# Layer 2's listed tiles in groups with one common range of nodes, added in PSUM by TensorE

## The chip, the cores and the metric

The kernel runs on one core of a Trainium2 chip. The metric is the time of one launch in device microseconds (us), the median of several runs. The profile is of one further execution, which has a time of its own.

## The reference

A two-layer relational graph convolution with 10 relations, a residual and a layer norm, in float32. There are N = 12,500 nodes with C = 128 features and E = 200,000 edges, sorted by their target `dst`. An edge's relation is the argmax of 10 of its 42 attributes. The weight of an edge's message is one over the number of edges with its target and relation.

```python
def _rgcn_layer(x, src, dst, edge_type, w_rel, root, bias):
    N = x.shape[0]
    seg = dst * NUM_REL + edge_type
    xs = x[src]
    sums = jax.ops.segment_sum(xs, seg, num_segments=N * NUM_REL)
    cnt = jax.ops.segment_sum(jnp.ones(seg.shape, x.dtype), seg, num_segments=N * NUM_REL)
    mean = (sums / jnp.maximum(cnt, 1.0)[:, None]).reshape(N, NUM_REL, -1)
    return jnp.einsum('nrd,rdo->no', mean, w_rel) + x @ root + bias

edge_type = jnp.argmax(msg[:, NODE_EMB_DIM:-NODE_EMB_DIM], axis=1)
h = jax.nn.relu(_rgcn_layer(x, src, dst, edge_type, w_rel1, root1, b1))
out = _layernorm(x + _rgcn_layer(h, src, dst, edge_type, w_rel2, root2, b2))
```

## The kernel before

Edges are cut into 1563 tiles of 128. **Layer 1** gathers each tile's source rows with an indirect DMA from GpSimd (L814), builds a one-hot tile on VectorE (`hots`, L821), whose row is an edge, whose column is a pair of node and relation in a short window of nodes, and whose entry is the edge's weight. TensorE multiplies the two (L1058) and VectorE adds the window into an accumulator of sums (`sum_into`, L847) at an offset that it loads into a register (`offsets`, L832). A finished block of 256 nodes is projected. Layer 1 also gathers the new features of source nodes that are already finished and sums them for layer 2 in the same way; these sums wait in DRAM (`SD`).

**Layer 2** (`layer_2`) does what is left. For each finished node and relation a projected row lies in `YD`. First come 177 plain tiles, whose edges are used as they stand. Behind them come the *listed* tiles: of each of 127 rows of 11 tiles, only the edges whose source was not finished in time in layer 1 are left, and `brought_together` packs them on the chip, while the plain tiles run, into 678 tiles of 128 edges (`NT2`). `listed(c)` makes, for each chunk of 128 such tiles, the gather's indices `idxB`, the keys `keyB` (an edge's node minus its tile's first node), the weights `wB` and the tiles' first nodes `rowB`. A tile's edges span a number of nodes that the planner bounds by `width2(u)`, from the share of edges left (`dense`, 0.92 down to 0.08); a tile that spans more raises a flag, and a general path at the end computes everything anew. The list has two runs, tiles 0 to 488 and 489 to 677; `taken_in_turns` merges them by a debt (`owed`).

The work runs in *bunches* of up to four tiles, in an order fixed when the program is built (`bunches`). For bunch `p` the code issues:

- the one-hot tiles of bunch `p + AH` (three ahead) on VectorE, in one of seven buffers;
- a gather for each tile of bunch `p` on GpSimd, into six buffers `g` of eight tiles each (`gathers`); the order in a buffer turns round on each use, so the first gather into it waits for the last product of its former use;
- the products of bunch `p` on TensorE (L1570), each tile into columns of its own of one of five PSUM banks (`zy0` to `zy2`, `zq0`, `zq1`);
- the adds of bunch `p - BE` (two behind) into `acc2` on VectorE (L1599), one per tile, each at its own register offset, which is loaded for eight tiles at a time and set by a register step ("ISA", FUSED_REGOPS).

Between them lie: the saved sums of 46 blocks, loaded by SyncE (1280 KB each, two buffers) and projected by ten products into the bank `alone` (`seen`, L807), then added by VectorE (L1494); `begun` (L1470), which starts a block of `acc2`; and `finish`, which transposes a finished block on TensorE (L1504), adds `x` (L754), normalizes and stores. A block is finished as soon as the adds of the last bunch that can touch it are issued. All engines take their instructions in the written order.

Of the kernel before, what the change touches and what calls it, by code (L numbers as in the profile page):

```python
# [9 lines left out]
F32 = mybir.dt.float32  # L10
BF16 = mybir.dt.bfloat16
I32 = mybir.dt.int32
# [8 lines left out]
P = 128  # L21
# [3 lines left out]
WN = 12  # L25
KW = NREL * WN
WMAX = 120
G = 16
QB = 4
GB = 6  # L30
# [10 lines left out]
YB = 512  # L41
# [26 lines left out]
def rgcn_resnorm_kernel(ctx: ExitStack, tc: tile.TileContext, x, src, dst, attr, w_rel1, root1, b1,  # L68
# [120 lines left out]
    def width2(u):  # L189

        a, b = rows_at(u, extent[u >= UX])
        w = max(row_width(r) for r in range(a, b + 1))
        assert w <= WMAX
        return w

    const = ctx.enter_context(tc.tile_pool(name="const", bufs=1))
    dram = ctx.enter_context(tc.tile_pool(name="dram", bufs=1, space=DRAM))
# [1115 lines left out]
    def listed(c):  # L1313
# [17 lines left out]
        nc.tensor.transpose(ps[:, :p], s_f[:p], ident[:p, :p])  # L1331
        nc.vector.tensor_scalar(si[:p], ki[:p], 4, None, op0=ALU.arith_shift_right)
        b = comp.tile([P, 4], F32, name="bB")
        bi = comp.tile([P, 1], I32, name="biB")

        def by_tile(to, vals):
            nc.vector.memset(to, float(vals[0]))
            for i in range(1, p):
                if vals[i] != vals[i - 1]:
# [3 lines left out]
        nc.vector.tensor_reduce(b[:p, 0:1], si[:p], axis=AX.X, op=ALU.max)  # L1343
        nc.vector.tensor_scalar(b[:p, 0:1], b[:p, 0:1], reach_of[1][:p, c:c + 1], reach_of[0][:p, c:c + 1],
                                op0=ALU.max, op1=ALU.min)
        nc.vector.tensor_scalar(bi[:p], b[:p, 0:1], -1.0, float(TOPN), op0=ALU.mult, op1=ALU.add)
        nc.scalar.dma_start(rowB[:, u0:u0 + p], bi[:p])
        key = comp.tile([P, P], F32, name="keyb")
        nc.vector.tensor_scalar(key[:p], si[:p], -1.0, b[:p, 0:1], op0=ALU.mult, op1=ALU.add)
        yield 1  # L1350
        nc.vector.tensor_copy(idxB[:, u0:u0 + p], ps[:, :p])
# [3 lines left out]
        nc.vector.tensor_scalar(v[:p], la[:p], 0.5, None, op0=ALU.is_gt)  # L1355
        nc.vector.tensor_tensor(dn[:p], key[:p], v[:p], op=ALU.mult)
        nc.vector.tensor_reduce(b[:p, 1:2], dn[:p], axis=AX.X, op=ALU.max)
        by_tile(b[:, 2:3], [width2(u) - 0.5 for u in range(u0, u0 + p)])
        nc.vector.tensor_tensor(b[:p, 1:2], b[:p, 1:2], b[:p, 2:3], op=ALU.is_gt)
        nc.vector.tensor_tensor(fl[:p], fl[:p], b[:p, 1:2], op=ALU.max)  # L1360
        nc.vector.tensor_scalar(li[:p], li[:p], P - 1, None, op0=ALU.bitwise_and)
# [20 lines left out]
    def layer_2():  # L1382

        def units(a, b):
            u, r = a, []
            while u < b:
                w = width2(u)
                n = 1
                while u + n < b and n < min(QB, YB // w) and width2(u + n) == w:
                    n += 1  # L1390
                r.append((True, u, n, w))
                u += n
            return r

        walks = [units(0, UX), units(UX, NT2)]

        def taken_in_turns(mean):
            rest = [list(walk) for walk in walks]
            order = []
            while sum(u[2] for u in order) < LEAD:  # L1400
                order.append(rest[0].pop(0))
            end = []
            while sum(u[2] for u in end) < LAST:
                end.insert(0, rest[0].pop())
            owed = 0.0
# [124 lines left out]
        for p in range(-AH, NB + BE):  # L1530
# [21 lines left out]
            if p < NB:  # L1552
                second, t0, n, w = bunches[p]
                oh = ohs.pop(p)
                zps[p] = zp = next_of("zp", banks)
                for j in range(n):
                    if made % GQ == 0:
                        g = next_of("g", gathers)
                        turn = used_[id(g)] = 1 - used_.get(id(g), 1)
                    at = GQ - 1 - made % GQ if turn else made % GQ  # L1560
                    made += 1
                    t = t0 + j
                    if second:
                        gathered(g, at, YD[:, :], idxB[:, t:t + 1], 1)
                    else:
                        gathered(g, at, YD[:NREL * (limit_of(t) + 1), :] if t >= T0 else YD[:, :], idxE[:, t:t + 1], 1)
                    gs[j] = g, at
                for j in range(n):
                    g, at = gs.pop(j)
                    nc.tensor.matmul(zp[:, j * w:(j + 1) * w], g[:, at * C:(at + 1) * C], oh[:, j * w:(j + 1) * w],  # L1570
                                     start=True, stop=True)
                i = issued[p + 1]
            if flag is None and i >= NG - 28 * QB:
                assert not jobs.due
# [8 lines left out]
                    seen_in(j)  # L1583
            for q in [q for q in sorted(zps) if q <= p - (1 if p >= NB - 4 else BE)]:
                second, t0, n, w = bunches[q]
                for j in range(n):
                    t = t0 + j
                    if (second, t) not in offs:
                        if second:
                            m = min(GB2, (UX if t < UX else NT2) - t)  # L1590
                            assert {t // P, (t + m - 1) // P} <= ready
                            vals = offsets(rowB[:, t:t + m], t, m, bounds2, False)
                        else:
                            m = min(GB2, (NX if t >= T0 else T0) - t)
# [4 lines left out]
                    nc.vector.tensor_tensor(s, s, zps[q][:, j * w:(j + 1) * w], op=ALU.add)  # L1599
# [177 lines left out]
```

## Time and profile before

| | |
|---|---|
| time, median of 3 runs | 3716.18 us (3711.78 to 3717.28) |
| time of the profiled execution | 3674.72 us |
| its span, first to last instruction | 3672.9 us |
| mean granted TensorE clock | 0.747 |
| busy: PE, DVE, ACT, POOL | 62%, 56%, 14%, 62% |
| listed tiles' gathers, first to last start | 2639.9 to 3629.3 us |
| gathers of listed tiles | 678, mean 947 ns |

PE is TensorE's matmul, PEld its weight load, DVE VectorE, ACT ScalarE, POOL GpSimd, SP SyncE; a name with a q is an engine's sequencer. A row of a group of instructions gives line, engine, operation, tiles (out<-in), shapes and count, then busy time and the mean of one in ns, then the engine's idle time just before them and what ended it. A row of the timeline gives start and duration, and in brackets the idle time before it. "issue" means that the engine waited for nothing that the profile shows, "remote" that the releaser is not in it. A row of the waits gives who waited for whom, the total in us, the times and the longest.

### The profile page before, as it was taken

To read this page: it belongs to the slowest core of one execution; us is meant where nothing else is said; L and a number is where in the kernel's file an instruction comes from. 1 tells how busy PE (TensorE), PEld (TensorE's weight loads), DVE (VectorE), ACT (ScalarE), POOL (GpSimd) and SP (SyncE) were. 2 spreads that over 40 slices of the span, in tenths; PEclk is the share of its full clock that TensorE was granted. 3 is DMA by queue.
4 is the path that set the end of the run, shared out by engine and by line. 5 is a ranking of instruction groups with operands and counts; after the bars stand their busy time and mean duration, and the time that the engine had idled before them with its cause. 6 is when DMAs were issued, how large, how long until landed. Compare 5 with 4: busy or idle time off the path is not lost.

```text
span 3672.9 us, 39395 instructions
## 1 busy us (share of the span) xinstructions
PE 2278.8 (62%) x11107; PEld 1884.6 (51%) x11107; DVE 2042.8 (56%) x6834; ACT 514.7 (14%) x799; POOL 2293.4 (62%) x2430
## 2 busy tenths in 40 slices
PE   1557676767676767666667677633556567666533
PEld 0445555555555655555555555523455456555533
DVE  4646576767565756575656565438653234333344
ACT  1111121212121212121212121100000000000000
POOL 5664666666666666666666666566566666666663
PEclk7677887888888888888888877855667666776655
DMA  4553655455555555555555555531234444444321
GB/s 121 156 166 100 191 158 189 151 190 160 187 165 176 171 171 174 170 173 174 178 174 174 161 162 160 149 82 52 70 103 138 134 132 145 141 145 133 86 61 43
DMA packets 377189, 529.35 MB, mean 144 GB/s; under 512 B 56664, under 2 KB 284467, under 8 KB 376964
## 3 DMA queue, kind: packets, MB, share of 16 engines
q0 software_dynamic: 99552, 249.45, 23.7%
q1 hardware_dynamic: 249209, 264.48, 22.2%
q10 hardware_dynamic: 28203, 12.82, 1.2%
q8 instruction: 92, 1.51, 0.2%
q14 instruction: 133, 1.09, 0.1%
HBM read 372.75 MB, written 160.19 MB: 145 GB/s over the span
## 4 chain that ended last, share of the span: by engine, by line
PE 18%; DVE 12%; issue 11%; another core or an unknown queue 9%; POOL 1%; DVEq 1%; ACT 1%; DMA 0%; SPq 0%; POOLq 0%; ACTq 0%
PE alone L807 5%; PE zp L1058 4%; DVE oh L821 3%; DVE cc L1599 3%; PE zy L1570 2%; PE pf L807 2%; PE yb L915 2%; POOL g L814 1%; PE zq L1570 1%; DVE cc L847 1%; DVEq L832 1%; DVE cc L1261 1%; PE pf L1296 1%; DVE go L1249 0%
## 5 line engine op out<-in xcount | busy, mean ns | idle before, releaser
L814 POOL DMA_INDIRECT g<-XH,idxE x1386 | 1313.9, 948 | 737.8 <-issue 364.9
L1058 PEld LDWEIGHTS zp<-oh,g 128*128 128x128 f32 x5898 | 901.9, 230 | 399.0 <-DVE cc L847 177.1
L1058 PE MATMUL zp<-oh,g 128*128 128x120 f32 x5898 | 943.4, 317 | 238.5 <-DVE cc L847 135.2
L847 DVE TENSOR_TENSOR cc<-cc,zp 128x240 f32 (+1 forms) x1563 | 606.5, 388 | 791.3 <-remote 317.6
L814 POOL DMA_INDIRECT g<-YD,idxB x678 | 641.9, 947 | 348.8 <-issue 193.2
L915 PE MATMUL yb<-w,a 128*128 128x512 f32 (+1 forms) x576 | 347.9, 694 | 343.4 <-ACT ys L921 176.7
L821 DVE TENSOR_SCALAR oh<-bank,keyE,wE 128x120 f32<-128x120 f32 x1563 | 517.5, 393 | 0.0
L807 PE MATMUL alone<-cc,w 128*128 128x256 f32 (+2 forms) x920 | 302.9, 498 | 93.9 <-issue 64.1
L1570 PE MATMUL zy<-oh,g 128*128 128x12 f32 (+20 forms) x1158 | 217.6, 324 | 198.7 <-DVE cc L1599 124.2
L921 ACT ACTIVATE ys<-yb 128x512 f32<-128x512 f32 (+2 forms) x291 | 153.0, 526 | 1325.4 <-remote 534.1
L1570 PEld LDWEIGHTS zy<-oh,g 128*128 128x128 f32 x1158 | 222.4, 278 | 210.7 <-DVE cc L1599 128.4
L807 PEld LDWEIGHTS alone<-cc,w 128*128 128x128 f32 x920 | 233.7, 270 | 147.3 <-issue 75.5
L915 PEld LDWEIGHTS yb<-w,a 128*128 128x128 f32 x576 | 110.6, 239 | 377.6 <-ACT ys L921 198.3
L807 PE MATMUL pf<-cc,w 128*128 128x256 f32 (+2 forms) x1040 | 247.1, 395 | 17.1 <-issue 8.3
L814 POOL DMA_INDIRECT g<-in_x_dram,idxE x177 | 167.6, 947 | 134.9 <-PE zp L1058 62.6
L814 POOL DMA_INDIRECT g<-YD,idxE x177 | 168.4, 951 | 114.7 <-issue 59.7
L807 PEld LDWEIGHTS pf<-cc,w 128*128 128x128 f32 x1040 | 205.3, 211 | 50.8 <-issue 15.7
L776 ACT ACTIVATE cc<-zero 128x1280 f32<-128x1280 f32 x170 | 214.5, 1262 | 0.0
L1599 DVE TENSOR_TENSOR cc<-cc,zy 128x12 f32 (+22 forms) x579 | 102.5, 177 | 181.1 <-remote 87.9
L821 DVE TENSOR_SCALAR oh<-columns,keyB,wB 128x15 f32<-128x15 f32 (+26 forms) x678 | 159.6, 319 | 0.0
L754 DVE TENSOR_TENSOR cc<-pf,x 128x256 f32<-128x256 f32 (+2 forms) x52 | 21.2, 408 | 227.2 <-remote 94.2
L1570 PE MATMUL zq<-oh,g 128*128 128x15 f32 (+26 forms) x552 | 98.6, 319 | 63.6 <-issue 28.4
(257 smaller groups left out, 1567.8 us busy)
## 6 DMA issues: line engine op xcount, KB each, us to landing
SD<-cc SPq DMA_DIRECT2D x41, 1280.0 KB
cc<-SD SPq DMA_DIRECT2D x41, 1280.0 KB
YD<-ys SPq DMA_DIRECT2D x194, 256.0 KB
m<-in_edge_attr_dram SPq DMA_DIRECT2D x48, 672.0 KB
g<-XH,idxE POOLq DMA_INDIRECT x1386
YD<-ys SPq DMA_DIRECT2D x97, 128.0 KB
XH<-hb SPq DMA_DIRECT2D x44, 256.0 KB
g<-YD,idxB POOLq DMA_INDIRECT x678
```

Of the source, the lines that this page charges most:

```text
L776: nc.scalar.activation(cc[:, l, h * H:(h + 1) * H, o:o + n], zero[:, None, :n].to_broadcast([P, H, n]), AF.Copy)
L807: nc.tensor.matmul(po[:, :n], wsb[l][:, r, :], sums[:, r], start=(r == 0), stop=(w is None and r == NREL - 1))
L814: nc.gpsimd.indirect_dma_start(out=g[:, j * C:(j + n) * C], out_offset=None, in_=table, in_offset=bass.IndirectOffsetOnAxis(ap=idx, axis=0))
L821: nc.vector.tensor_scalar(oh[:, j * m:(j + 1) * m], cols[:, :m], keys[:, j:j + 1], weights[:, j:j + 1], op0=ALU.is_equal, op1=ALU.mult)
L832: vals = nc.values_load_multi_w_load_instructions(row, engines=[DVE], min_val=min(a for a, _ in lims), max_val=max(b for _, b in lims), sk ...
L847: nc.vector.tensor_tensor(s, s, z, op=ALU.add)
L915: nc.tensor.matmul(yb[:h, :m], fin_a[k][:, b * P:b * P + h], wsb[1][:, r:r + m // C, :], start=True, stop=True)
L921: nc.scalar.activation(ys[:h, :m], yb[:h, :m], AF.Copy)
L1058: nc.tensor.matmul(zp[:, o + l * KW:o + (l + 1) * KW], g[:, (slot[j] + l) * C:(slot[j] + l + 1) * C], oh[:, j * KW:(j + 1) * KW], start=Tr ...
L1261: nc.vector.copy_predicated(to[:, c - m:EW - m], go[:, c - KW:], a[:, c:])
L1570: nc.tensor.matmul(zp[:, j * w:(j + 1) * w], g[:, at * C:(at + 1) * C], oh[:, j * w:(j + 1) * w], start=True, stop=True)
L1599: nc.vector.tensor_tensor(s, s, zps[q][:, j * w:(j + 1) * w], op=ALU.add)
```

## The change

`group_at` joins listed tiles that follow each other into groups of four, else of two, else one, where the group's common range of nodes fits 120 columns: 38.6 over the smallest `dense` plus 2.99 for four, 20.8 for two, the old width for one. A group is a bunch. All its tiles have one first node, the group's, and one width; TensorE adds the group's products in the same columns of PSUM, and VectorE adds the columns once. `listed` therefore finds the group's first node across tiles, which lie in partitions: a transpose to one partition, a maximum over each group, a copy back over the group, and a small matmul back to partitions. `rowB` is now written by VectorE, where a DMA of ScalarE's queue did it. Two more steps of `QB` tiles lie in `listed`. The debt of the merge counts the add once per bunch.

```diff
+GROUPS = ((4, 38.6), (2, 20.8))
...
+    def group_at(u, end):
+
+        for n, m in GROUPS:
+            if u % P + n <= P and u + n <= end:
+                a, b = rows_at(u, extent[u >= UX])[0], rows_at(u + n - 1, extent[u >= UX])[1]
+                if a:
+                    w = int(m / min(dense[a * RT:(b + 1) * RT]) + 2.99)
+                    if w <= WMAX:
+                        return n, w
+        return 1, width2(u)
+
+    groups2, u = [], 0
+    while u < NT2:
+        n, w = group_at(u, UX if u < UX else NT2)
+        groups2.append((u, n, w))
+        u += n
+    width_of = {u + j: w for u, n, w in groups2 for j in range(n)}
...
-        bi = comp.tile([P, 1], I32, name="biB")
+        key = comp.tile([P, P], F32, name="keyb")
+        firsts, lasts = key[0:1], dn[0:1]
...
-        nc.vector.tensor_scalar(bi[:p], b[:p, 0:1], -1.0, float(TOPN), op0=ALU.mult, op1=ALU.add)
-        nc.scalar.dma_start(rowB[:, u0:u0 + p], bi[:p])
-        key = comp.tile([P, P], F32, name="keyb")
+        nc.tensor.transpose(ps[0:1, P:P + p], b[:p, 0:1], ident[:p, :p])
+        yield 1
+        runs = []
...
+        for a, n, m in runs:
+            to = firsts[:, a:a + m * n]
+            if n == 1:
+                nc.vector.tensor_copy(to, ps[0:1, P + a:P + a + m])
+            else:
+                nc.vector.tensor_reduce(lasts[:, :m], ps[0:1, P + a:P + a + m * n].rearrange("p (m n) -> p m n", n=n), axis=AX.X, op=ALU.max)
+                nc.vector.tensor_copy(to.rearrange("p (m n) -> p m n", n=n), lasts[:, :m, None].to_broadcast([1, m, n]))
+        nc.tensor.matmul(ps[:p, 2 * P:2 * P + 1], firsts[:, :p], ident[0:1, 0:1], start=True, stop=True)
+        nc.vector.tensor_scalar(rowB[:, u0:u0 + p], firsts[:, :p], -1.0, float(TOPN), op0=ALU.mult, op1=ALU.add)
+        yield 1
+        nc.vector.tensor_copy(b[:p, 0:1], ps[:p, 2 * P:2 * P + 1])
...
-        by_tile(b[:, 2:3], [width2(u) - 0.5 for u in range(u0, u0 + p)])
+        by_tile(b[:, 2:3], [width_of[u] - 0.5 for u in range(u0, u0 + p)])
...
         def units(a, b):
-            u, r = a, []
-            while u < b:
-                w = width2(u)
-                n = 1
-                while u + n < b and n < min(QB, YB // w) and width2(u + n) == w:
-                    n += 1
-                r.append((True, u, n, w))
-                u += n
-            return r
+            return [(True, u, n, w) for u, n, w in groups2 if a <= u < b]
...
-                owed = min(owed + u[2] * (mean - 3 * u[3] - 125), mean)
+                owed = min(owed + u[2] * (mean - 3 * u[3] / u[2] - 125), mean)
...
-                    nc.tensor.matmul(zp[:, j * w:(j + 1) * w], g[:, at * C:(at + 1) * C], oh[:, j * w:(j + 1) * w],
-                                     start=True, stop=True)
+                    o = 0 if second else j * w
+                    nc.tensor.matmul(zp[:, o:o + w], g[:, at * C:(at + 1) * C], oh[:, j * w:(j + 1) * w],
+                                     start=not second or j == 0, stop=not second or j == n - 1)
...
-                for j in range(n):
+                for j in range(1 if second else n):
                     t = t0 + j
```

What this makes of the engines' order is shown at two places. The first is VectorE near the end of the list, where all bunches have four tiles. Before (L821 the one-hot tiles, L832 the load of eight offsets, ISA the register step, L1599 the adds):

```order
L1599 TENSOR_TENSOR cc<-cc,zq_17236 128x24
L832 TENSOR_LOAD rowB
L1599 ISA
L1599 TENSOR_TENSOR cc<-cc,zq_17236 128x24
L1599 ISA
L1599 TENSOR_TENSOR cc<-cc,zq_17236 128x24
L1599 ISA
L1599 TENSOR_TENSOR cc<-cc,zq_17236 128x24
L821 TENSOR_SCALAR oh_96<-columns,keyB,wB 128x25 x4
```

And now, at the same stretch of the list (L840, L851 and L1629 are the same three lines):

```order
L851 TENSOR_LOAD rowB
L1629 ISA
L1629 TENSOR_TENSOR cc<-cc,zq_17203 128x75
L840 TENSOR_SCALAR oh_97<-columns,keyB,wB 128x78 x4
L1629 ISA
L1629 TENSOR_TENSOR cc<-cc,zq_17204 128x75
L840 TENSOR_SCALAR oh_98<-columns,keyB,wB 128x82 x4
```

Four adds and four register steps of a bunch have become one each, and the one-hot tiles and the add are about three times as wide.

The second place is TensorE in the middle, where the two runs of the list are mixed. Before (L1570 the products, L807 the ten products of the saved sums, L1470 the start of a block):

```order
L807 MATMUL alone<-cc,w_391 128x256 x10
L1570 MATMUL zq_17236<-oh_94,g_86 128x74
L1570 MATMUL zq_17236<-oh_94,g_87 128x74 x3
L1470 MATMUL pf<-cc,root_393 128x256
L1570 MATMUL zy_15678<-oh_95,g_87 128x16 x4
L1570 MATMUL zy_15679<-oh_96,g_87 128x16
L1570 MATMUL zy_15679<-oh_96,g_88 128x16 x3
L807 MATMUL alone<-cc,w_391 128x256 x10
```

And now (L1600, L826, L1533 and L1499 stand for L1570, L807, L1504 and L1470):

```order
L1600 MATMUL zy_15678<-oh_98,g_90 128x74
L1600 MATMUL zy_15679<-oh_92,g_91 128x51 x4
L826 MATMUL alone<-cc,w_391 128x256 x10
L1600 MATMUL zy_15680<-oh_93,g_91 128x74
L1600 MATMUL zq_17203<-oh_94,g_91 128x51 x3
L1600 MATMUL zq_17203<-oh_94,g_86 128x51
L1533 MATMUL pf<-ident,cc 128x128 x2
L1499 MATMUL pf<-cc,root_393 128x256
L1600 MATMUL zq_17204<-oh_95,g_86 128x74
```

Tiles of the second run, which had been taken four at a time, now stand alone, each with a PSUM bank of its own, between groups of four of the first run.

More of the change, by code (lines that the diff above doesn't have):

```diff
@@ L1345, in listed @@
                                 op0=ALU.max, op1=ALU.min)
-        nc.vector.tensor_scalar(bi[:p], b[:p, 0:1], -1.0, float(TOPN), op0=ALU.mult, op1=ALU.add)
-        nc.scalar.dma_start(rowB[:, u0:u0 + p], bi[:p])
-        key = comp.tile([P, P], F32, name="keyb")
+        nc.tensor.transpose(ps[0:1, P:P + p], b[:p, 0:1], ident[:p, :p])
+        yield 1
+        runs = []
+        for u, n, _ in groups2:
+            if u0 <= u < u0 + p:
+                if runs and runs[-1][1] == n:
+                    runs[-1][2] += 1
+                else:
+                    runs.append([u - u0, n, 1])
+        for a, n, m in runs:
+            to = firsts[:, a:a + m * n]
+            if n == 1:
+                nc.vector.tensor_copy(to, ps[0:1, P + a:P + a + m])
+            else:
+                nc.vector.tensor_reduce(lasts[:, :m], ps[0:1, P + a:P + a + m * n].rearrange("p (m n) -> p m n", n=n), axis=AX.X, op=ALU.max)
[4 more added lines that the diff above has]
+        nc.vector.tensor_copy(b[:p, 0:1], ps[:p, 2 * P:2 * P + 1])
         nc.vector.tensor_scalar(key[:p], si[:p], -1.0, b[:p, 0:1], op0=ALU.mult, op1=ALU.add)
```

## The prediction

> **What bounds the kernel now.** I began with the busy time of the engines by stage. The listed tiles of layer 2, which the change touches, start at about 2640 us and last nearly to the end of the 3672.9 us span.
>
> ```profile
> 2000.00:2100.00 100.00, 71.76 (x395) 58.11 (x394) 60.94 (x176) 19.92 (x29) 65.44 (x69) 0.86 0.51 157
> 2900.00:3000.00 100.00, 56.43 (x245) 47.89 (x245) 37.73 (x186) 4.10 (x11) 60.57 (x64) 0.68 0.44 130
> 3500.00:3600.00 100.00, 34.59 (x151) 32.07 (x151) 36.35 (x184) 1.48 (x5) 67.51 (x72) 0.50 0.24 61
> ```
>
> The columns are the window, its length, then PE, PEld, DVE, ACT and POOL busy (with counts), the granted clock, the DMA share and GB/s. No engine is full in the listed stage. VectorE is busy for about 37 us of 100, TensorE for 35 to 56. So the next view is that of GpSimd, which issues one gather per tile: the group of its gathers from the page, and one stop in the timeline.
>
> ```profile
> L814 POOL DMA_INDIRECT g<-YD,idxB x678 | 641.9, 947 | 348.8 <-issue 193.2
> ...
> 2904.45 0.94 POOL L814 DMA_INDIRECT g<-YD,idxB  x1 [4.82 <-issue]
> 2905.69 0.95 POOL L814 DMA_INDIRECT g<-YD,idxB  x1 [0.30 <-issue]
> 2906.94 0.95 POOL L814 DMA_INDIRECT g<-YD,idxB  x1 [0.30 <-issue]
> ```
>
> Undisturbed, a gather follows a gather after 0.95 + 0.30 = 1.25 us. The 678 gathers would take 848 us, of which 203 us would be idle. The row has 348.8 us idle, so GpSimd stands still for about 145 us more. It stops, as at 2904 us, in front of a gather whose buffer TensorE has not yet read. GpSimd is the floor under this stage, but it is held back by the engines that consume what it gathers. What holds those back is in the chain of work that ended last, cut to this stage (1033 us), and in the waits.
>
> ```profile
> by line: issue 19.4%; another core or an unknown queue 18.5%; PE alone L807 18.1%; DVE cc L1599 7.4%; PE zy L1570 6.9%; DVE oh L821 6.6%; PE zq L1570 3.6%; POOL g L814 2.8%; DVEq L832 2.1%; DVE st L757 1.5%; PE pf L1470 1.4%; DVE cc L754 1.
> ...
> PE pf L1504 <- DVE cc L1599: 116.9, 23, 25.6
> DVE cc L1599 <- remote: 67.4, 22, 6.6
> DVE cc L1599 <- DVE cc L1599: 48.3, 60, 1.3
> ```
>
> The adds of the tiles' products (L1599) are 7.4% of the chain, 76 us, and TensorE's transposes of a finished block waited 117 us for them. An add itself waits in two ways: for a releaser that the profile does not name ("remote", 22 times, 3.06 us each), and for the add before it, 60 times. The timeline of VectorE while GpSimd issues without pause shows both:
>
> ```profile
> 3613.13 0.18 DVE L1599 TENSOR_TENSOR cc<-cc,zy 128x23 f32 x1 [2.01 <-remote]
> 3613.83 0.18 DVE L1599 TENSOR_TENSOR cc<-cc,zy 128x23 f32 x1 [0.52 <-DVE cc L1599]
> 3615.26 0.18 DVE L1599 TENSOR_TENSOR cc<-cc,zy 128x23 f32 x1 [1.25 <-DVE cc L1599]
> ...
> 3616.03 0.18 DVE L1599 TENSOR_TENSOR cc<-cc,zy 128x23 f32 x1
> ```
>
> Four adds of 0.18 us each take 3.1 us, because each waits for a signal. The stage is bound by hand-overs between TensorE and VectorE, with GpSimd's 1.25 us a tile as the floor.
>
> **The change part by part.** The planner's rules (written out with the sizes of this case) give 216 bunches of listed tiles in place of 182: 141 of four tiles, 39 of two and 36 of one. The widths, summed over tiles, rise from 18,423 to 46,372 columns; the adds' widths fall from 18,423 to 15,888, since there is one add per bunch.
>
> ```profile
> L821 DVE TENSOR_SCALAR oh<-columns,keyB,wB 128x15 f32<-128x15 f32 (+26 forms) x678 | 159.6, 319 | 0.0
> L1599 DVE TENSOR_TENSOR cc<-cc,zy 128x15 f32 (+23 forms) x448 | 81.0, 181 | 129.9 <-remote 46.1 <-issue 40.8 <-DVE cc L1599 32.7
> L1599 DVE TENSOR_TENSOR cc<-cc,zq 128x15 f32 (+26 forms) x276 | 51.3, 186 | 82.1 <-remote 21.3 <-issue 19.1 <-DVE cc L1599 15.7
> ...
> L821 DVE TENSOR_SCALAR oh<-columns,keyB,wB 128x15 f32<-128x15 f32 x85 | 19.2, 313 | 0.0
> L821 DVE TENSOR_SCALAR oh<-columns,keyB,wB 128x119 f32<-128x119 f32 x17 | 4.7, 350 | 0.0
> L1599 DVE TENSOR_TENSOR cc<-cc,zq 128x15 f32 x32 | 5.4, 169 | 2.8 <-issue 1.8 <-DVE cc L1599 0.3
> L1599 DVE TENSOR_TENSOR cc<-cc,zq 128x119 f32 x8 | 2.2, 279 | 5.7 <-PE zy L1570 5.5
> ```
>
> *Adds.* Busy time over count is 0.169 us at 15 columns and 0.275 at 119, so 1.0 ns a column on 0.153 us. Now the 724 adds of this stage (46 of them plain tiles) are busy 132 us, the listed ones 124. After: 216 x 0.153 + 15,888 x 1.0 ns = 49 us, 40% of it. Of the 76 us on the chain, 678/724 are listed, 71 us, and 60% of that is 43 us. **Taken: -43.** If the adds only fill time in which VectorE would wait anyhow, it is 0; at most the whole 75 us of busy time goes.
>
> *Waits of an add for the add before.* In the order of the instructions 735 of 855 adds now hold such a wait, and 260 after. Of the 48.3 us the share 1 - 260/735 is 31 us. VectorE has slack in most of this stage, so half is counted. **Taken: -16**, ends 0 and -31.
>
> *Wider one-hot tiles.* 19.2/85 = 0.226 us against 4.7/17 = 0.276 us gives 0.48 ns a column; 27,949 columns more cost 13 us of 160. They are 68 us of the chain, so **+6**, ends 0 and +13.
>
> *Products.* Each tile keeps its two weight loads and two matmul rows, only wider, and now adds in PSUM. Three rows of the timeline, the first and the last of eight matmuls each, with one granted clock over all three:
>
> ```profile
> 2956.56 0.98 PE L1570 MATMUL zy<-oh,g 128*128 128x40 f32 x8
> 2957.37 4.56 PE L807 MATMUL alone<-cc,w 128*128 128x256 f32 x20
> 2961.77 0.96 PE L1570 MATMUL zy<-oh,g 128*128 128x15 f32 x8
> ```
>
> [...] **Taken: 0.** [...]
>
> *The listing.* Per chunk of 128 tiles a transpose, a small matmul, about half a dozen copies and reductions on one partition, and more steps of the width table come in; a DMA on ScalarE's queue goes. Beyond the adds and their register steps VectorE's order grows by about 95 instructions. At 0.16 us, as the smallest of this stage, that is 15 us.
>
> ```profile
> L1341 DVE TENSOR_TENSOR bB<-bB 128x1 f32<-128x1 f32 x27 | 4.4, 162 | 1.6 <-DVE bB L1340 0.5 <-issue 0.2
> 2500.00:2600.00 100.00, 31.75 (x134) 29.32 (x134) 81.46 (x205) 2.42 (x4) 62.68 (x67) 0.50 0.19 51
> 2600.00:2700.00 100.00, 62.66 (x269) 52.81 (x269) 61.86 (x281) 3.84 (x10) 53.10 (x56) 0.69 0.25 71
> ```
>
> They fall where VectorE is 62 to 81% busy, so half is counted: **+7**, ends 0 and +15. The two more steps in which a chunk waits push it back by eight gathers, 10 us; the chunk is needed later than that, and if it were not, one such delay is the price.
>
> *The order of bunches.* Two runs through the list are still merged by a debt; its count now charges the add once per bunch, so the mix shifts. The last 40 tiles, the gathers and the loads of the saved sums stay. Five bunches, the number of PSUM banks, hold 14 tiles in most of the mixed part where they held 16 to 20. That shortens TensorE's lead over VectorE. GpSimd's lead (six buffers of eight tiles, refilled eight at a time, so 40 tiles) covers it, so I take 0; the upper end is the slower rival below.
>
> Sum: -43 - 16 + 6 + 7 = -46 us. The profiled execution took 3674.7 us, so it would take 3629. The timed runs' median, 3716.2 us, lies 41.5 us above that execution; the same difference from the median gives **3670 us**. The ends of the terms give -75 - 31 = -106 at best and +28 at worst. When these waits go, TensorE's products for the saved sums (L807, 18% of the chain) and the unnamed releasers are late next, which is why I do not count more.
>
> **The rivals.** *GpSimd becomes the bound.* Fewer signals per tile could let TensorE keep up altogether. All 145 us of GpSimd's stops go, giving 3571 us. For it: stops of this size occur in every part of the stage, with TensorE at 56% and at 35%, so load does not set them and signals may. Against it: the unnamed releases at L1494 and L754 are not touched.
>
> *No gain.* The adds lie beside other waits and the time stays at 3716, within 0.2%, 7.4 us, about what a measurement of this kernel can tell from no change. For it: VectorE idles 60% of the stage. Against: the 117 us that transposes wait for adds.
>
> *Columns cost TensorE time.* If the wide products cost per column what L807 does, 4.56 us/20/256 = 0.89 ns, two rows of 27,949 columns are 50 us, and -46 becomes +4: 3720 us. The equal rows at 15 and 40 columns leave it little. [...]
>
> *Slower: hand-overs set the pace, not adds.* There are 34 more bunches, each a release of VectorE by TensorE, and bunches of one or two tiles shrink the lead. If each new hand-over costs the 3.06 us of the mean unnamed wait, 34 x 3.06 = 104 us, against -46: 3774 us. It decides from 15 of the 34 on (46/3.06). For it: a stop of 25 us in which both engines wait on each other is in the trace. Against it: most bunches are as long as before, and each releases with one add.
>
> *The change does not do what it says.* A group wider than its common range would raise the flag and start the general path, whose two layers gather 1600 tiles each, over 3.0 ms more by 0.95 us a gather. Worked out from the inputs, the fullest group uses 0.88 of its width: under 0.01.
>
> **How the numbers follow.** Forecast, -15 to -90 us (3626 to 3701): 0.52. GpSimd as the bound: 0.15. No gain: 0.08. Columns: 0.03. Slower hand-overs: 0.22. Faster is 0.52 + 0.15 = 0.67, same 0.08 + 0.03 = 0.11, slower 0.22. The range takes the forecast, the two cases near zero, the upper half of the GpSimd case (from 3590) and the lower part of the slower one (to 3740): 0.52 + 0.11 + 0.08 + 0.10 = 0.81. The forecast's own range is 3626 to 3701.
>
> **What would show it.** Right: adds at about 216 in this stage plus the plain ones, near 50 us busy; waits of an add for an add at a third of 48 us; GpSimd's idle time down by some 46 us, with its gathers still 1.25 us apart. TensorE's rows as fast at 75 columns as at 23. Wrong: GpSimd's idle time unchanged or larger while adds are fewer, which would mean that the releases and not the adds count; or wide matmul rows that take longer, which would mean columns; or a stage before 2640 us that changed by more than the listing's few microseconds.

## The result and the profile after

The changed kernel took 3686.45 us (3683.29 to 3694.06), the kernel before beside it 3709.4 us (3703.7 to 3717.28): a ratio of 0.9941, interval 0.9926 to 0.9956, about 22 us less. The forecast was 3670 us, 46 us less. Less than half of it came, and not where the prediction put it.

The runs stood on several chips, and these are of two kinds. On the chips of the runs above and on three others the kernel before takes 3685 to 3721 us; on three more it takes 3072 us, 17% less, with the same instructions. I call them late and prompt chips; the last section shows why. The whole change was run on late chips only. On prompt chips its parts were run (groups in the tail, groups everywhere else, the listing without groups), and none of them changed the time by more than 0.1%.

Where the time went is read from marks that both traces have: GpSimd's first gather of a plain tile, its first and last gather of a listed tile, and VectorE's last instruction. Four rows of the timeline of the kernel before:

```profile
2358.23 0.94 POOL L814 DMA_INDIRECT g<-YD,idxE  x1 [1.75 <-PE zp L1058]
2639.92 0.94 POOL L814 DMA_INDIRECT g<-YD,idxB  x1 [0.30 <-issue]
3629.28 0.94 POOL L814 DMA_INDIRECT g<-YD,idxB  x1 [0.30 <-issue]
3667.13 0.34 DVE L764 TENSOR_SCALAR o<-cc,mv,rstd 128x128 f32<-128x128 f32 x1
```

and the same four of the changed kernel:

```profile
2388.36 0.94 POOL L833 DMA_INDIRECT g<-YD,idxE  x1 [2.87 <-PE zp L1077]
2665.51 0.94 POOL L833 DMA_INDIRECT g<-YD,idxB  x1 [0.30 <-issue]
3655.57 0.94 POOL L833 DMA_INDIRECT g<-YD,idxB  x1 [0.30 <-issue]
3679.95 0.35 DVE L783 TENSOR_SCALAR o<-cc,mv,rstd 128x128 f32<-128x128 f32 x1
```

The plain stage (first plain to first listed gather) went from 281.7 to 277.1 us, the listed stage (first to last listed gather) from 989.4 to 990.1, the tail behind the last gather from 38.2 to 24.7. That is -4.6 + 0.7 - 13.5 = -17.4 us; some 5 of the 22 us are not placed by it. The first mark lies 30 us later, in a part that the change doesn't touch. In the experiments it stands at 2363 to 2366 us on the two chips where before takes 3685 us, at 2391 to 2398 us on the one where it takes 3721; so the profiled execution of before, with 2358 us, was probably not on the same chip as the timed runs beside it. With 3674.72 us it is also faster than every timed run of that kernel (3703.7 us at least), so what its stages differ by from those of the changed kernel is uncertain by several us. A second trace of the changed kernel (run e8 below) has 994.4 us of listed stage and a tail of 24.9. The tail is the firmest of the three differences: another trace with single adds at the end (adds doubled, below) has 37.5 us.

The groups, the chain of work by line and the waits of the changed kernel, cut to 2640 to 3686 us:

```profile
L833 POOL DMA_INDIRECT g<-YD,idxB x678 | 641.2, 946 | 350.1 <-issue 189.2 <-remote 71.7 <-PE zy L1600 51.2
L840 DVE TENSOR_SCALAR oh<-columns,keyB,wB 128x45 f32<-128x45 f32 (+35 forms) x678 | 176.7, 332 | 0.0
L1629 DVE TENSOR_TENSOR cc<-cc,zy 128x12 f32 (+29 forms) x191 | 39.8, 208 | 99.5 <-remote 49.3 <-PE zy L1600 20.1 <-issue 12.8
L1629 DVE TENSOR_TENSOR cc<-cc,zq 128x48 f32 (+33 forms) x87 | 20.1, 231 | 80.1 <-remote 47.0 <-issue 15.7 <-PE zy L1600 10.2
...
by line: issue 18.9%; another core or an unknown queue 17.6%; PE alone L826 12.6%; POOL g L833 8.4%; PE zy L1600 5.8%; PE zq L1600 4.3%; DVE oh L840 3.5%; PE pf L1533 1.3%; PE pf L1499 1.1%; DVE st L776 0.9%; DVE cc L1629 0.9%; DVE cc L773 
...
DVE cc L773 <- remote: 121.0, 12, 17.4
DVE cc L1523 <- remote: 110.9, 10, 21.9
DVE cc L1629 <- remote: 96.3, 17, 16.3
PE pf L1533 <- DVE cc L1629: 80.9, 17, 16.3
DVE cc L1629 <- DVE cc L1629: 2.0, 3, 1.1
```

The adds fell to 278 with 59.9 us busy, the waits of an add for an add from 48.3 to 2.0 us, the adds' share of the chain from 7.4% to 0.9%. GpSimd's idle time in its listed gathers is where it was, 348.8 and 350.1 us. In place of the adds' own time stand longer waits of VectorE for the releaser that the profile does not name. In the kernel before it waited for that releaser 67.4 us at the adds (L1599), and at the two other lines

```profile
DVE cc L1494 <- remote: 96.0, 13, 14.2
DVE cc L754 <- remote: 89.6, 10, 25.7
```

253 us in all. Now it is 121.0 + 110.9 + 96.3 = 328 us. The sum varies from trace to trace: 398 us in the second trace of the changed kernel, 277 us in each of two kernels below that have half of the grouping, 201 us with adds doubled. So the direction fits in all of them, and the size is not shown.

### The profile page after: what moved, and what is told of

Read it like the earlier page. It is cut to its first block, busy times and chain, and to the rows that moved or that the text cites. A ratio compares the mean times of both kernels' runs of the same rounds, so it can differ in the third digit from the quotient of the medians.

```text
span 3685.9 us, 38579 instructions
## 1 busy us (share of the span) xinstructions
PE 2296.4 (62%) x11125; PEld 1886.5 (51%) x11125; DVE 1995.4 (54%) x6434; ACT 513.5 (14%) x799; POOL 2287.9 (62%) x2430
## 5 line engine op out<-in xcount | busy, mean ns | idle before, releaser
L833 POOL DMA_INDIRECT g<-YD,idxB x678 | 641.2, 946 | 350.1 <-issue 189.2
L840 DVE TENSOR_SCALAR oh<-bank,keyE,wE 128x120 f32<-128x120 f32 x1563 | 517.7, 394 | 0.0
L826 PE MATMUL alone<-cc,w 128*128 128x256 f32 (+2 forms) x920 | 291.7, 480 | 103.5 <-issue 54.6
L1600 PE MATMUL zy<-oh,g 128*128 128x12 f32 (+30 forms) x1168 | 230.5, 346 | 175.2 <-DVE cc L1629 97.1
L1600 PEld LDWEIGHTS zy<-oh,g 128*128 128x128 f32 x1168 | 227.5, 280 | 191.0 <-DVE cc L1629 103.0
L826 PEld LDWEIGHTS alone<-cc,w 128*128 128x128 f32 x920 | 223.7, 258 | 156.2 <-issue 68.2
L826 PE MATMUL pf<-cc,w 128*128 128x256 f32 (+2 forms) x1040 | 255.3, 402 | 20.6 <-issue 15.2
L826 PEld LDWEIGHTS pf<-cc,w 128*128 128x128 f32 x1040 | 209.0, 215 | 59.5 <-issue 29.4
L840 DVE TENSOR_SCALAR oh<-columns,keyB,wB 128x45 f32<-128x45 f32 (+35 forms) x678 | 176.7, 332 | 0.0
L773 DVE TENSOR_TENSOR cc<-pf,x 128x256 f32<-128x256 f32 (+2 forms) x52 | 21.2, 409 | 222.3 <-remote 121.0
L1629 DVE TENSOR_TENSOR cc<-cc,zy 128x12 f32 (+24 forms) x306 | 58.8, 192 | 152.6 <-remote 83.6
L1600 PE MATMUL zq<-oh,g 128*128 128x45 f32 (+33 forms) x542 | 101.2, 337 | 44.2 <-issue 39.3
```

Of the source, the lines that this page charges most:

```text
L773: nc.vector.tensor_tensor(v[:p, s], pr[:p, s], xb[:p, s], op=ALU.add)
L826: nc.tensor.matmul(po[:, :n], wsb[l][:, r, :], sums[:, r], start=(r == 0), stop=(w is None and r == NREL - 1))
L833: nc.gpsimd.indirect_dma_start(out=g[:, j * C:(j + n) * C], out_offset=None, in_=table, in_offset=bass.IndirectOffsetOnAxis(ap=idx, axis=0))
L840: nc.vector.tensor_scalar(oh[:, j * m:(j + 1) * m], cols[:, :m], keys[:, j:j + 1], weights[:, j:j + 1], op0=ALU.is_equal, op1=ALU.mult)
L1600: nc.tensor.matmul(zp[:, o:o + w], g[:, at * C:(at + 1) * C], oh[:, j * w:(j + 1) * w], start=not second or j == 0, stop=not second or j = ...
```

## The experiments

**The theories.** D (drain): while GpSimd issues, VectorE has slack and the adds cost nothing; only behind the last gather, when TensorE and VectorE work off what has been gathered, are they on the path. A (adds): they are on the path all through the listed stage, as the prediction had it. O (order): the gain comes from the new listing and the order that it shifts. The first expectations count the tail to the end of the span, 43.6 us before and 30.3 after; the later ones, and this text, to VectorE's last instruction.

*Groups in the last 41 tiles only.* The rule that forms a group gets one condition more. The rest of the edit, not shown, gives the tiles that are in no group the bunches, the columns of PSUM, the adds and the debt of before.

```diff
-            if u % P + n <= P and u + n <= end:
+            if UX - LAST - 1 <= u < UX and u % P + n <= P and u + n <= end:
```

> The changed kernel, but only the last 41 listed tiles of the first run go in groups; all other listed tiles go one by one, as before. The change gave -22 us in the timed runs; in its one profile the time from the last gather to the end fell by 13 us (43.6 to 30.3) and the stage of listed gathers did not move (989.4 to 990.1 us). Theory D (drain): adds are on the path only after GpSimd's last gather, so nearly all of the gain is here: -13 to -22 us against the kernel before, and a tail near 30 us. Theory A (adds are on the path all through the listed stage): these are 41 of 678 tiles, 6% of the gain: -1 to -3 us. Theory O (the gain comes from the new listing and order ahead of the listed stage): about -5 us, with a tail of 43 us.

Measured beside a before of 3072.62 us: 3071.78 us, 0.9996 (0.9987 to 1.0004). No theory's number came: the chip was a prompt one.

*Groups everywhere but there.* The same condition with a `not`.

> The changed kernel, but its last 41 listed tiles of the first run go one by one, as before; all others go in groups. Theory D: the gain is in the drain, so little is left here: 0 to -8 us, and a tail near 43 us. Theory A: 94% of the gain stays: -19 to -22 us. Theory O: about -5 us in the plain stage, and nothing in the listed one.

3071.07 us, 0.9998 (0.9989 to 1.0006).

*Adds doubled outside the tail*, in the kernel before:

```diff
                     nc.vector.tensor_tensor(s, s, zps[q][:, j * w:(j + 1) * w], op=ALU.add)
+                    if second and q < NB - 11:
+                        nc.vector.tensor_tensor(s, s, zero[:, :w], op=ALU.add)
```

> The kernel before, with a second add after every add of a listed tile, of zeros and to the same place, except in the last 11 bunches: some 640 adds more, which by their 0.18 us are 115 us of VectorE, and as many waits of an add for an add. Theory D: VectorE has slack while gathers run, so the stage of listed gathers stays at 989 us and the time within 10 us of the kernel before. Theory A, by the terms of the prediction (71 us of adds on the chain and half of 48 us of waits, all doubled): 70 to 95 us slower. If the extra adds bite only where VectorE is fullest, something in between, and the windows show where.

3072.28 us, 0.9997 (0.9987 to 1.0006): 636 adds more at no cost.

*The kernel before, a second profile.*

> The kernel before once more, for a second profile of it. If the tail of 43.6 us, the 989 us of listed gathers and GpSimd's 349 us of idle time belong to the kernel and not to one execution, they come again within 3 us, 10 us and 10 us; the first gather of a plain tile, at 2358 us in the profile shown and at 2388 us in that of the changed kernel, shows how much the part ahead varies from execution to execution.

3069.31 us. The expectation missed by far, and the miss explains the three runs above. The group of gathers, the chain from 2202 us on and the waits:

```profile
L814 POOL DMA_INDIRECT g<-YD,idxB x678 | 640.3, 944 | 206.6 <-issue 190.5 <-DMA g<-YD,idxB 6.1 <-PE zy L1570 3.7
...
by line: POOL g L814 33.8%; PE alone L807 17.5%; issue 16.5%; DMA g<-YD,idxB 15.1%; PE zy L1570 4.9%; PE zq L1570 2.3%; DVE oh L821 1.1%; DVE cc L1599 0.7%; PE pf L1504 0.7%; DMA cc<-hT 0.7%; PE pf L1470 0.7%; DVE st L757 0.4%; DVE bB L1341
...
DVE cc L1494 <- PE alone L807: 131.6, 26, 10.8
DVE cc L754 <- PE pf L1504: 189.4, 39, 11.5
```

Of 206.6 us idle 203 are the 0.30 us between gathers: GpSimd never stops. The listed stage takes 845.6 us, the floor of 1.25 us a tile, and its tail 14.0 us. No wait of this stretch has an unnamed releaser. Where gathers alone set the pace, adds could be taken away in part or doubled, and the time stayed.

*The changed kernel again, and few gathers.* In the second and third kernel here only the first tile of a bunch gathers, and one that begins a buffer; the others use its rows. So these two leave out a part of the work, and their output is another.

```diff
-                    if second:
+                    if second and j and g is gs[0][0]:
+                        at = gs[0][1]
+                    elif second:
                         gathered(g, at, YD[:, :], idxB[:, t:t + 1], 1)
```

> The changed kernel itself once more. Beside the first experiments the kernel before took 3073 us, not the 3709 to 3716 us of the runs shown, and in its trace GpSimd's gathers of listed tiles never stop (206.6 us idle, 203 of it the 0.30 us between gathers). Theory G (where the kernel runs in 3073 us the gathers alone set the pace of the listed stage): within 4 us of the kernel before, 846 us of listed gathers, a tail of 12 to 15 us. Theory A (adds on the path): -20 us or more. Where the kernel before takes 3709 us again: -22 us by both, as measured.

> The kernel before; of a bunch's listed tiles only the first gathers (and one that begins a new buffer), the others use its rows, so that the output is another. Some 200 gathers in place of 678. Theory G: with the floor of 1.25 us a tile gone, the listed stage falls from 846 us to what TensorE needs there, 390 to 450 us by its busy time: 400 to 450 us off the whole. Theory A: the adds and their hand-overs hold the stage, and it falls by less than 150 us.

> The changed kernel with the same left out: of a bunch's listed tiles only the first gathers, the others use its rows. It shows what the change is worth where gathers do not set the pace. Theory H (adds and their waits are then on the path, as the prediction costed them): 40 to 60 us less than the kernel before with few gathers. Theory T (TensorE's own work is the bound then, and VectorE still has slack): within 10 us of it. Theory C (wider products cost time per column where TensorE is the bound): up to 50 us more.

This chip was a late one, before 3721.15 us. The changed kernel: 3698.96 us, 0.9946 (0.9929 to 0.9964), the first result again; plain, listed and tail are 279.0, 994.4 and 24.9 us. Few gathers: 3381.27 us (0.9085, 0.9068 to 0.9103) and with the change 3367.35 us (0.9047, 0.9029 to 0.9064). So 347 gathers fewer (331 of 678 stayed, more than the 200 expected, since many bunches begin a buffer) take 340 us off, 0.98 us each. G's 400 to 450 us were not reached. With half of the gathers gone the change is worth 14 us, between theory T's 10 and H's 40 to 60 and nearer to T. The changed kernel has eight gathers more here; at 0.98 us each, equal numbers would make it about 22 us (an estimate).

```profile
L814 POOL DMA_INDIRECT g<-YD,idxB x331 | 312.3, 943 | 335.9 <-PE zy L1572 122.6
...
by line: PE alone L807 26.9%; issue 12.6%; DVE oh L821 9.4%; DVE cc L1601 8.4%; PE zy L1572 7.2%; another core or an unknown queue 4.9%; PE zq L1572 4.8%; DVEq L832 2.9%; DVE st L757 2.1%; PE pf L1470 2.1%; DVE cc L754 1.9%; DVE o L764 1.9%
```

These are the gathers and the chain from 2670 us on of the kernel before with few gathers: GpSimd now waits for TensorE by name, and the products for the saved sums (L807) lead the chain with 26.9%. The unnamed releaser has 4.9% of the chain, where the kernel before has 18.5%. So fewer gathers shorten the stage on a late chip too, but whether by their own time or because fewer signals come late, this run doesn't tell. The tail went from 51.7 to 29.0 us with the change, the listed stage from 647.0 to 659.6 us.

*Tail only and adds doubled, again.*

> Again the changed kernel with groups in the last 41 listed tiles of the first run only, for a chip on which the kernel before takes about 3715 us (the first such run stood beside a before of 3073 us). There the change was measured at -22 us twice, with the tail after the last gather at 24.7 and 24.9 us where before had 38.2, and listed gathers of 990 and 994 us where before had 989. Theory D (drain): -11 to -22 us, tail near 26 us. Theory A (adds on the path all through the stage): -1 to -3 us. Theory O (the new listing and order): -5 us, tail 38 us. If before takes 3073 us again: no difference.

> Again the kernel before with a second add of zeros after every add of a listed tile, except in the last 11 bunches, some 640 more adds of 0.18 us. Theory D (VectorE has slack while gathers run): within 10 us of the kernel before also where that takes about 3715 us, listed gathers of 985 to 1000 us. Theory A, by the prediction's terms: 70 to 95 us slower, nearly all of it in the listed stage. If before takes 3073 us again: no difference, as measured.

A late chip, before 3685.05 us. Groups in the tail alone: 3669.42 us, 0.9957 (0.9943 to 0.9972), -16 us. Adds doubled: 3703.99 us, 1.0060 (1.0046 to 1.0075), +22 us by the ratio. The doubled adds are 636 more with 121.1 us busy:

```profile
L814 POOL DMA_INDIRECT g<-YD,idxB x678 | 641.7, 946 | 359.8 <-issue 193.4 <-remote 81.5 <-PE zy L1570 46.8
...
L1601 DVE TENSOR_TENSOR cc<-cc,zero 128x15 f32 (+25 forms) x636 | 121.1, 190 | 134.1 <-remote 50.8 <-DVE cc L1599 50.3 <-issue 14.0
```

So a microsecond of adds costs about 22/121 = 0.18 us on a late chip. Theory A wanted 70 to 95 us, D under 10: both miss, D by less. The listed stage is 1000.3 us here and the idle time of GpSimd 359.8, both 11 us more than in the trace of the kernel before. This trace is of the fastest of the six executions, 3689.09 us.

The tail-only kernel makes D's time and not D's way: its tail is 34.2 us, not 26, only 4.0 us less than before; plain and listed stage are 278.3 and 984.4 us.

*The listing with no groups.* The condition is `False`.

> The changed kernel with no groups at all: the new listing of the blocks' tiles (through TensorE and a row on VectorE, without the DMA of the start positions on ScalarE's queue) stays, every listed tile has its own width and its own add, and bunches are as in the kernel before. On a chip on which before took 3685 us, groups in the last 41 tiles only gave -16 us, but the tail after the last gather fell by only 3 us there, and the stages before it by 3 to 5 us each. Theory O (the missing DMA and the shifted steps give part of the gain): -8 to -16 us. Theory D (the gain is in the drain): within 4 us of the kernel before, or up to 7 us slower by the listing's extra steps. If before takes 3073 us: no difference by both.

A prompt chip: 3073.75 us, 1.0008 (0.9999 to 1.0017), which tells nothing of the late ones.

*All but the tail, twice more.*

> Again the changed kernel with its last 41 listed tiles of the first run one by one, all others in groups. On chips on which before took 3685 to 3721 us the whole change gave -22 us, and the new listing with groups in the tail alone -16 us; so groups outside the tail are worth about -6 us, and what this kernel shows beyond that is the listing's. Theory D (drain): the listing is worth nothing, so -3 to -9 us here, with a tail near 37 us. Theory O (the listing and its order give the -16): -18 to -24 us, tail near 37 us. If before takes 3073 us: no difference, as measured.

A prompt chip: 3070.40 us, 0.9996 (0.9987 to 1.0005).

> Once more the changed kernel with its last 41 listed tiles of the first run one by one, all others in groups, since the two runs of it so far stood beside a before of 3072 us. Where before takes 3685 to 3721 us, theory D (drain): -3 to -9 us, with a tail near 37 us and listed gathers within 10 us of 989. Theory O (the new listing and its order give what the tail alone seemed to give): -18 to -24 us, tail near 37 us. If before takes 3073 us again: no difference.

A late chip, before 3686.26 us: 3667.03 us, 0.9958 (0.9944 to 0.9971), -16 us by the ratio, -19 by the medians. Its listed stage is 988.7 us, its plain stage 274.5, and its tail 27.0, against both theories' 37, though the tiles of the tail have their single adds.

What the tails consist of is seen from where TensorE's last product of a listed tile stands. The last gather and that product, in the kernel with groups in the tail only:

```profile
3628.47 0.95 POOL L833 DMA_INDIRECT g<-YD,idxB  x1 [0.30 <-issue]
3654.05 0.47 PE L1612 MATMUL zy<-oh,g 128*128 128x26 f32 x2
```

and with groups everywhere but in the tail:

```profile
3627.67 0.94 POOL L833 DMA_INDIRECT g<-YD,idxB  x1 [0.30 <-issue]
3642.26 1.32 PE L1612 MATMUL zy<-oh,g 128*128 128x26 f32 x6
```

TensorE reaches the last tile (in the second row the last two of six matmuls) 25.6 us behind its gather in the one and 15.3 in the other. In the kernel before it is 25.9, with adds doubled 25.0, in the changed kernel 15.7 and 15.9. So 10 us of TensorE's arrears are gone in the three traces with groups outside the tail, and in none of the three without. How long GpSimd has issued without a stop is not what does it: its last stop is in front of the 7th last gather both with adds doubled (25.0 us) and with groups everywhere but in the tail (15.3). The grouping and the order of bunches that comes with it are not told apart. From that product to the end it is 12.3 and 12.5 us with single adds, 11.7 with groups outside the tail only, 8.6, 9.0 and 9.0 with groups in the tail: the adds there are worth 3.4 us.

Where single adds stand in these arrears is seen in the timeline of the kernel before, around its last gather. Adds of 23 columns belong to tiles ahead of the last 41, whose widths are 24 to 26, and so to those that are single with groups in the tail only and grouped with groups everywhere else:

```profile
3622.26 0.18 DVE L1599 TENSOR_TENSOR cc<-cc,zy 128x23 f32 x1 [1.92 <-remote]
3623.18 0.18 DVE L1599 TENSOR_TENSOR cc<-cc,zy 128x23 f32 x1
3629.96 0.18 DVE L1599 TENSOR_TENSOR cc<-cc,zy 128x23 f32 x1 [6.60 <-remote]
3631.36 0.18 DVE L1599 TENSOR_TENSOR cc<-cc,zy 128x23 f32 x1 [1.22 <-DVE cc L1599]
3632.76 0.18 DVE L1599 TENSOR_TENSOR cc<-cc,zy 128x23 f32 x1 [1.22 <-DVE cc L1599]
3633.48 0.47 PE L1504 MATMUL pf<-ident,cc 128*128 128x128 f32 x1 [10.67 <-DVE cc L1599]
3633.75 4.73 PE L1570 MATMUL zy<-oh,g 128*128 128x24 f32 x22
```

The adds of a finished block come one at a time, four of the five rows behind a wait of 1.22 to 6.60 us; TensorE's transpose waits 10.67 us for the last of them, and 11 tiles' products stand behind it. With groups in the tail only the same transpose waits 7.59 us for such adds. In the chain of the last 88 us of before and of the last 86 us after, the adds went from 22.6% to 2.6%:

```profile
by line: another core or an unknown queue 24.0%; DVE cc L1599 22.6%; issue 11.2%; DVE oh L821 8.0%; PE zy L1570 5.1%; PE pf L1504 3.5%; DVE cc L754 3.4%; DVE st L757 3.3%; DVE o L764 3.2%; ACT rstd L760 3.1%; DVEq L832 2.8%; PE zq L1570 2.7
...
by line: issue 24.8%; POOL g L833 18.6%; PE zy L1600 7.4%; DVE oh L840 6.4%; another core or an unknown queue 5.3%; PE zq L1600 4.8%; DVE st L776 3.7%; DVE cc L773 3.4%; DVE o L783 3.2%; PE pf L1533 2.8%; DVE mv L777 2.6%; DVE cc L1629 2.6%
```

**What stays open.** The two halves of the grouping gave -16 us each by their ratios, the whole -20 to -22, so they don't add up. Either both hold something in common, which by the sum of the ratios would be worth 10 us (with an uncertainty of about 9), or the second half finds little left, or the chips differ: the halves were measured where before takes 3685 us, the whole where it takes 3709 and 3721, and no set of runs has both. What the halves share is the new listing and its order. For it stands the plain stage, which holds no listed add: 281.7, 281.5 and 283.8 us in three traces of late chips with the old listing, 274.5 to 279.0 in five with the new. On prompt chips the plain stage shows no such difference: 227.9 and 228.2 us with the old listing, 225.5 to 229.3 with the new. The listing by itself was run on a prompt chip only, so its worth on a late chip is not shown, and how the 22 us divide between tail, listing and order stays open.

## Why the prediction was right, and where it wasn't

Sign and range were right (3590 to 3740 held 3686, and so did the forecast's own 3626 to 3701), the size and the place were not. That the narrower range held is in part luck: the part of the gain that the traces place is mostly the tail's, and the prediction had no term for the tail. By its steps:

*The bound.* That GpSimd is the floor, "held back by the engines that consume what it gathers", fits the late chips; on a prompt one nothing holds it back, and the listed stage takes 845.6 us, the floor. That the adds were the hand-overs that held it back was wrong: the sign that the prediction named for this, GpSimd's idle time unchanged while adds are fewer, is what came (348.8 to 350.1 us).

*Adds, -43, and waits of adds for adds, -16.* These are the terms that failed. Their working was right: 59.9 us busy with some plain ones, and 48.3 us of waits fell to 2.0, more than the two thirds forecast. But the share of the chain was counted as if it all came off. The prediction gave the bound itself, that adds may "only fill time in which VectorE would wait anyhow": in the listed stage they mostly do. It changed by 0.7 us in the two traces, and 121 us of adds put in cost 22 us. What the traces place is in the tail, 13.5 us: 10 of arrears and 3.4 of the last adds.

*One-hot tiles, +6.* Busy time rose by 17.1 us (159.6 to 176.7) where 13 was forecast. No run tells how much of it is on the path.

*Products, 0.* Nearly right. Eight matmuls at 26 columns in the tail of the kernel before, with the window's granted clock (0.50):

```profile
3650.04 1.91 PE L1570 MATMUL zq<-oh,g 128*128 128x26 f32 x8
...
3650.00:3660.00 10.00, 4.26 (x18) 3.54 (x17) 6.76 (x34) 0.59 (x2) 0.00 (x0) 0.50 0.08 20
```

and at 78 columns in that of the changed one, under the same clock:

```profile
3641.59 1.99 PE L1600 MATMUL zq<-oh,g 128*128 128x78 f32 x8 [2.79 <-DVE cc L1629]
3645.11 1.83 PE L1600 MATMUL zq<-oh,g 128*128 128x78 f32 x8
...
3641.00:3647.00 6.00, 4.62 (x20) 4.12 (x20) 3.79 (x18) 0.00 (x0) 4.48 (x6) 0.50 0.34 94
```

Three times the columns cost 1.83 to 1.99 us against 1.91. At the 0.89 ns of the rival of columns, an estimate from the row of L807, they would have cost 0.37 us more, so it is out. What sets the pace of such a product no run shows. In the trace of the kernel before, where the granted clock is 1.00 (2956 to 2963 us), eight took 0.98 us at 40 columns and 0.96 at 15, and their weight loads 1.08 us at both. Over all products of layer 2, plain tiles included, the pages of the profile have, before and after:

```profile
L1570 PE MATMUL zy<-oh,g 128*128 128x12 f32 (+20 forms) x1158 | 217.6, 324 | 198.7 <-DVE cc L1599 124.2
L1570 PE MATMUL zq<-oh,g 128*128 128x15 f32 (+26 forms) x552 | 98.6, 319 | 63.6 <-issue 28.4
...
L1600 PE MATMUL zy<-oh,g 128*128 128x12 f32 (+30 forms) x1168 | 230.5, 346 | 175.2 <-DVE cc L1629 97.1
L1600 PE MATMUL zq<-oh,g 128*128 128x45 f32 (+33 forms) x542 | 101.2, 337 | 44.2 <-issue 39.3
```

The same 1710 matmuls are busy 331.7 us instead of 316.2. So the wider products are not quite free, 15.5 us of TensorE's time; that any of it lengthened the kernel is not shown.

*Listing, +7.* The sign was wrong or the term is nothing: the plain stage got 5 us shorter on late chips, and the listing alone cost nothing clear on a prompt one (1.0008).

*The order of bunches, 0.* Open, as said above.

*The rivals.* GpSimd as the bound (3571): not on late chips, where its stops stayed. On prompt chips it is the bound, and there the parts of the change are worth nothing. Slower hand-overs (3774): the 34 more bunches didn't cost 3.06 us each. "No gain" was nearest to the mechanism in the listed stage. The step from one execution to the median, +41.5 us, was probably a step from one chip to another.

## What to carry to other kernels

A share of the chain of waits is what an operation occupies, not what its removal returns. Here the chain was full of releases that it can't name, the adds fell from 7.4% to 0.9% of it, and the stage stayed as long; what the traces place of the gain lies mostly behind the last gather. Before costing such a stage, ask whether the idle time of the engine that paces it will move. And double the suspected cost on the chip before removing it: 121 us of extra adds cost 22, so taking away some 70 would hardly have brought the 59 that were forecast for adds and their waits (at that rate it is 13, an estimate).

## What the runs showed of the hardware

Chips differ by 17% in this kernel, with the same instructions: 3072 us on three, 3685 to 3721 on four sets of runs. No chip is known to have been met twice; that it is the chip that differs is what these sets suggest. Durations agree (the mean gather of a listed tile takes 943 to 947 ns in the traces of late chips, 944 to 946 in four of prompt ones). The mean granted clock does not, 0.747 against 0.794, but the same twenty products take 5.83 us on a late chip and 5.89 on a prompt one in the rows below. What differs there is when finished work is noticed. On a late chip, in the kernel before (the letters SPq mark the queue of SyncE):

```profile
2765.57 5.83 PE L807 MATMUL alone<-cc,w 128*128 128x256 f32 x20
...
2779.46 0.94 POOL L814 DMA_INDIRECT g<-YD,idxB  x1 [0.30 <-issue]
2783.29 0.52 SPq L1484 DMA_DIRECT2D cc<-SD  x1
2783.30 0.42 DVE L1494 TENSOR_TENSOR cc<-cc,alone 128x256 f32<-128x256 f32 x1 [14.18 <-remote]
2783.87 0.94 POOL L814 DMA_INDIRECT g<-YD,idxB  x1 [3.46 <-remote]
```

and on a prompt one, in the same kernel:

```profile
2488.67 5.89 PE L807 MATMUL alone<-cc,w 128*128 128x256 f32 x20
...
2494.60 0.42 DVE L1494 TENSOR_TENSOR cc<-cc,alone 128x256 f32<-128x256 f32 x1 [1.10 <-PE alone L807]
```

There VectorE goes on 0.04 us after TensorE's last matmul; here 11.9 us after it, together with SyncE and GpSimd, 2.9 us after GpSimd's last gather had ended. GpSimd had issued without pause up to then. The trace also has events of each engine's counter. VectorE's at 2768.43 us comes 0.01 us after the end of the one-hot tile before it; TensorE's first one after these products comes at 2783.27 us, and SyncE and VectorE go on 0.02 and 0.03 us behind it. On TensorE's counter, between 2690 and 3640 us of the kernel before, the first event after an instruction's end comes more than 1.5 us behind it 58 times, 348 us in all, and 71 times in the changed kernel, 361 us. On the prompt chip that happens twice in the whole execution, 1.8 us each. It is not TensorE alone: on VectorE's counter it happens 80 times in the same stretch of the kernel before (424 us), and never on the prompt chip. Some of these are instructions whose event is not in the trace: the stretch has 621 events for 703 instructions of TensorE that make one, and 633 for 1102 of VectorE. Of the 58, 35 (144 us) come more than 1.5 us even after the last such instruction that had ended, and of the 80, 13 (43 us).

So what the profile calls an unnamed releaser is here, as far as these events tell, an engine's own signal come late. They are not a full account: on the late chip TensorE's counter has 1993 events for 2294 instructions that make one, on the prompt chip 2286. Nor does a pause of GpSimd let the signals out in general: of the 58, 24 end in such a pause and 29 while a gather runs, and on the prompt chip GpSimd issues all through the stage and the signals are in time. Why they are late, and why on some chips only, no run here settles.
